# Attention by four heads and a block of keys: values and denominators on 32 columns per head, denominators in a bank of the scores

## Chip, cores, metric

One core of one Trainium2 chip. The metric is device microseconds (us) of one execution.

## The reference, cut to what matters

A graph layer and an attention layer, each with a residual and a layer norm, on a batch of 32 graphs of 512 nodes with 512 features, all in float32:

```python
def reference(x, adj, ...):                      # x (32, 512, 512), adj (512, 512)
    x = layernorm(x + gnn(x, adj))               # layer 0: deg * (x Wi + b) + adj (x Wj)
    q, k, v = heads(x @ Wq.T + bq), heads(x @ Wk.T + bk), heads(x @ Wv.T + bv)   # 8 heads of 64
    scores = einsum('bhqd,bhkd->bhqk', q, k) / 8
    scores = where(adj == 0, -inf, scores)
    attn = softmax(scores, axis=-1)
    out = einsum('bhqk,bhkd->bhqd', attn, v)
    return layernorm(x + out @ Wo.T + bo)
```

The kernel uses no maximum in the softmax. It takes exp(score), multiplies by a mask of 0 and 1, and divides the sum over keys of e·v by the sum of e (the *denominators*). A flag sum over denominators and reciprocals (`told`) decides at the end whether a safe version must run; with these inputs it does not.

## The kernel before: the parts that matter

One batch is eight *steps*. A step makes the scores of two blocks of 128 keys for one pair of heads, then the values of the step before, then some pieces of the projections of this and of neighbouring batches. The order on each engine is the order of the program. It allocates eight banks of PSUM, all in use: two for projections, two `ov` tiles of one bank, two `sc` tiles of two banks.

```python
def ov_tile():  return psum.tile([P, 512], FT, name="ov", bufs=2)
def sc_tile():  return psum.tile([P, 2, N], FT, name="sc", bufs=2)

def scores(b, hp, kc):                      # hp: pair of heads, kc: block of 128 keys
    ps = sc_tile()
    for s in range(2):
        nc.tensor.matmul(ps[:, s, :], KT[...], QT[...], start=True, stop=True)
    e = E[kc] = work([P, 2, N], "e", 4)
    nc.scalar.activation(ps, ps, AF.Exp, scale=QSCALE)
    nc.vector.tensor_tensor(e, ps, edge[...], op=OP.mult)          # the masking
...
def values(b, hp, half, kcs=None):          # two heads of 64 columns side by side
    if half == 0:
        PV[hp] = ov_tile()
    for kc in kcs or range(2 * half, 2 * half + 2):
        for s in range(2):
            c0 = hp * P + s * HD
            nc.tensor.matmul(PV[hp][s * HD:(s + 1) * HD, :], V[b][:, kc, c0:c0 + HD], E[kc][:, s, :], ...)

def sums(b, hp):                            # denominators of two heads, in an ov bank
    pl = ov_tile()
    for s in range(2):
        nc.tensor.matmul(pl[s * HD:(s + 1) * HD, :], ones[:, :HD], ES[hp][:, s, :], start=True, stop=True)
    RL[hp] = (pl, work([P, N], "rl", 1))

def rest(b, hp):                            # 4 reciprocals, scaling of the values, flag sum (tell)
    return [(invert, b, hp, c) for c in range(4)] + [(scale, b, hp), (tell, b, hp)]
...
for step in range(STEPS):
    hp, half = divmod(step, 2)
    scores(b, hp, 2 * half)
    scores(b, hp, 2 * half + 1)
    if step > 0:
        values(b, *divmod(step - 1, 2)) ; after a second half: sums(...), extra = rest(...)
    elif b > 0:
        values(b - 1, HP - 1, 1); sums(b - 1, HP - 1); extra = rest(b - 1, HP - 1)
    for f in PERIODS[n][step]:              # pieces of projections and their side work
        run(f)
        some = 0 if f[0] == 0.0 else len(extra) if step == 0 else max(1, round(f[0] / PC))
        # after a piece, `some` items of rest() are issued
```

The side work, cut from the lists of one batch: `base` is the residual base on VectorE (two inputs in SBUF), `combos`, `add_bo` and the first addition of `presum` are GpSimd's, `h_turn` is a transposition on VectorE.

```python
# phase_a(n), the end of a batch
    ... z(base, n, 0), z(combos, TX, n, xq, (3, 4)), z(combos, TA, n, aq, (3, 4)), z(base, n, 1), pc("l0", n, 1, A), k[4]]
# phase_b(n), the start of the next
    return [l0[2], *project(m, 1), l0[6], *project(m, 2), l0[7], z(add_bo, n - 1, 0), *project(m, 6), l0[4], z(stats, n, 0), ...
            l0[3], z(stats, n, 1), z(h_turn, n, 0), *project(m, 5)]
# phase_c(n), the middle
    ... q[1], k[1], z(apply, m, 0), q[2], z(apply, m, 1), z(store, m), z(h_turn, n, 1), z(combos, TH, n, h, (1, 2)), ...
```

Of the kernel before, what the change touches and what calls it, by code (L numbers as in the profile page):

```python
# [25 lines left out]
def gnn_attention_kernel(  # L26
# [16 lines left out]
):  # L43

# [114 lines left out]
    wo = load_w(work([P, NC, D], "xh", 3), woT, nc.sync)  # L159
# [17 lines left out]
    told = const.tile([P, B * HP + 1], FT, name="told")  # L177
# [31 lines left out]
    nc.gpsimd.dma_start(bv_c, bv.rearrange("(c p) -> p c", p=P))  # L209
# [4 lines left out]
    def graph_forms(part):  # L214
        if part == 3:
            nc.vector.reduce_sum(deg_c, adj_f, axis=AX.X)
        elif part == 0:
            nc.vector.tensor_tensor(adj_f, adjT, adjR.bitcast(FT), op=OP.not_equal)
        elif part == 1:
            nc.vector.reduce_sum(told[:, B * HP:], adj_f.rearrange("p c i -> p (c i)"), axis=AX.X)  # L220
            nc.vector.tensor_scalar(told[:, B * HP:], told[:, B * HP:], 2.0 * SAFE, None, op0=OP.mult)
        else:
            nc.vector.tensor_scalar(edge, adjT, 0.0, None, op0=OP.not_equal)


    RING = 8
# [5 lines left out]
    def combine(name, eng, part):  # L232
# [5 lines left out]
        if part == 0:  # L238
# [4 lines left out]
            made = ((6, s2), (5, s1), (3, s4))  # L243
        else:
# [8 lines left out]
    for name, src in (("wi", wiT), ("wj", wjT), ("wv", wvT), ("wq", wqT), ("wk", wkT), ("wo", woT)):  # L253
        WS[name, 1] = rows(src)[:, 0:2, 0:Q]
        WS[name, 2] = rows(src)[:, 2:4, 0:Q]
# [207 lines left out]
    def scores(b, hp, kc):  # L463
# [5 lines left out]
        e = E[kc] = work([P, 2, N], "e", 4)  # L469
# [4 lines left out]
    def presum(hp, half):  # L474

        if half == 0:
            ES[hp] = work([P, 2, N], "es", 1)
            nc.gpsimd.tensor_add(ES[hp], E[0], E[1])  # L478
        else:
            nc.vector.tensor_add(ES[hp], ES[hp], E[half])  # L480

    def values(b, hp, half, kcs=None):
        if half == 0:
            PV[hp] = ov_tile()
        for kc in kcs or range(2 * half, 2 * half + 2):
            for s in range(2):
                c0 = hp * P + s * HD
                nc.tensor.matmul(PV[hp][s * HD:(s + 1) * HD, :], V[b][:, kc, c0:c0 + HD], E[kc][:, s, :],  # L488
                                 start=(kc == 0), stop=(kc == NC - 1))

    def sums(b, hp):

        pl = ov_tile()
        for s in range(2):
            nc.tensor.matmul(pl[s * HD:(s + 1) * HD, :], ones[:, :HD], ES[hp][:, s, :], start=True, stop=True)  # L495
        RL[hp] = (pl, work([P, N], "rl", 1))

    def last_sums(hp, parts=(0, 2, 3)):

        if 0 in parts:  # L500
            RL[hp] = (ov_tile(), work([P, N], "rl", 1))
        for kc in parts:
            src = ES[hp] if kc == 0 else E[kc]
            for s in range(2):
                nc.tensor.matmul(RL[hp][0][s * HD:(s + 1) * HD, :], ones[:, :HD], src[:, s, :], start=(kc == 0), stop=(kc == 3))  # L505

    def invert(b, hp, part):
        pl, rl = RL[hp]
# [3 lines left out]
    def tell(b, hp):  # L512
        pl, rl = RL[hp]
        j = b * HP + hp
        nc.vector.tensor_tensor_reduce(pl, pl, rl, 1.0, 0.0, OP.add, OP.add, told[:, j:j + 1])

    def scale(b, hp, c=slice(0, N)):
        if hp % 2 == 0:
            OT[b, hp // 2] = work([P, 2, N], "oT", 3)
        nc.vector.tensor_mul(OT[b, hp // 2][:, hp % 2, c], PV[hp][:, c], RL[hp][1][:, c])  # L520

    def rest(b, hp):
        return [(invert, b, hp, c) for c in range(4)] + [(scale, b, hp), (tell, b, hp)]
# [150 lines left out]
    def last_steps():  # L674
# [4 lines left out]
        own = [(4 * GA, last_part, hp, 0) for hp in range(3)]  # L679
        return [[z(last_load), FLUSH, c[0], p[1], c[1]], [p[2], p[6]], [p[5], p[7], z(add_bo, B - 1, 0), z(add_bo, B - 1, 1)],  # L680
                [p[3], p[4], z(stats, m, 0), z(stats, m, 1)], [FLUSH, own[0], z(apply, m, 0), z(apply, m, 1), z(store, m)],
                [own[1]], [FLUSH, own[2]], []]
# [7 lines left out]
    def last_load():  # L690
        t = load_w(work([P, NC, D], "xh", 3), woT, nc.sync)
        W["wo"] = [t[:, 0:2, :], t[:, 2:4, :]]

    def last_part(hp, half=None, ic=None):
        if hp == 0:
# [5 lines left out]
        for ic in (range(2 * half, 2 * half + 2) if ic is None else (ic,)):  # L701
            nc.tensor.matmul(ACC[ic], OT[B - 1, hp // 2][:, hp % 2, ic * P:(ic + 1) * P], W["wo"][hp // 2][:, hp % 2, :],
                             start=(hp == 0), stop=(hp == HP - 1))
# [31 lines left out]
    for n in range(1, B + 1):  # L735
        b = n - 1
        extra = []
        for step in range(STEPS):
            hp, half = divmod(step, 2)
            scores(b, hp, 2 * half)  # L740
            scores(b, hp, 2 * half + 1)
            if step > 0:
                ph, phalf = divmod(step - 1, 2)
                values(b, ph, phalf)
                if phalf == 1:
                    last_sums(ph) if b == B - 1 else sums(b, ph)
                    extra = rest(b, ph)
            elif b > 0:
                values(b - 1, HP - 1, 1)
                sums(b - 1, HP - 1)  # L750
                extra = rest(b - 1, HP - 1)
            late = [(presum, hp, 0)] if half == 0 else [(presum, hp, 2), (presum, hp, 3)] if b < B - 1 else []
# [14 lines left out]
    last_sums(HP - 1, (0,))  # L767
    for kc in (2, 3):
        values(B - 1, HP - 1, 1, (kc,))
        last_sums(HP - 1, (kc,))  # L770
    for hp in range(HP - 1):
        last_part(hp, 1)
    for ic in range(NC):
        invert(B - 1, HP - 1, ic)
        scale(B - 1, HP - 1, slice(ic * P, (ic + 1) * P))
# [142 lines left out]
```

## Time and profile before

| | before |
|---|---|
| time, median of 3 | 3794.23 us (3789.84 to 3796.48) |
| TensorE busy | 99% |
| VectorE, GpSimd, ScalarE busy | 71%, 53%, 26% |
| length of one batch | 116.0 us, eight steps of 12.7 to 15.6 us |

TensorE's stream has practically no gap, so its length is the time. The prediction shows the lines. In those of a timeline the columns are the start, the length of a run of like instructions, engine, line, operation, output and inputs, shape and count; in brackets the idle time before it and what ended it. In those of groups they are busy time, the mean of one in ns, then the idle time before them and its main causes.

### The profile page before, as it was taken

The page shows a single profiled execution, that of the slowest core. Times are in us where ns is not written, and L with a number is a line of the kernel's source. Part 1 is how long each engine was busy: PE and PEld are TensorE (multiplying, and loading weights), DVE is VectorE, ACT ScalarE, POOL GpSimd, SP SyncE. Part 2 cuts the span into 40 slices and gives each one's busy share as a digit, 9 for nine tenths or more (in the row PEclk, how much of TensorE's full clock was granted, in tenths as well). Part 3 has the DMA queues.
Part 4 walks back from the last instruction along what each step waited for, and adds up shares of the span by engine and source line. Part 5 has one row for each costly group of instructions (what it writes and reads, how often), then busy time and mean ns, then how long its engine had stood idle before and what let it go on. Part 6 is the DMA issues. An engine that isn't in the chain of part 4 may idle for free.

```text
span 3793.4 us, 46029 instructions
## 1 busy us (share of the span) xinstructions
PE 3736.6 (99%) x16426; PEld 2551.5 (67%) x16426; DVE 2694.1 (71%) x3580; ACT 992.3 (26%) x1356; POOL 2027.6 (53%) x1985
## 2 busy tenths in 40 slices
PE   8999999999999999999999999999999999999997
PEld 5667666666666666666666666666666666666663
DVE  4677776777767777777777777777777777777765
ACT  2222222222222222222222222222222222222222
POOL 3556545656555565456555555654565545556533
PEclk9999999999999999999999999999999999999998
DMA  7444455445555445554445554455544555544540
GB/s 252 129 117 131 137 153 155 131 131 136 145 155 147 126 131 141 151 158 130 129 136 144 156 144 130 130 143 148 161 128 128 138 143 158 144 131 127 143 139 24
DMA packets 803720, 529.25 MB, mean 140 GB/s; under 512 B 529568, under 2 KB 626336, under 8 KB 803488
## 3 DMA queue, kind: packets, MB, share of 16 engines
q1 hardware_dynamic: 786912, 494.26, 47.7%
q10 hardware_dynamic: 16320, 31.46, 2.4%
q8 instruction: 135, 2.21, 0.2%
q14 instruction: 97, 0.79, 0.1%
q0 software_dynamic: 256, 0.53, 0.0%
HBM read 453.25 MB, written 72.88 MB: 139 GB/s over the span
## 4 chain that ended last, share of the span: by engine, by line
PE 92%; DVE 4%; POOL 1%; ACT 1%; DMA 1%; issue 1%; SPq 0%; DVEq 0%; POOLq 0%; ACTq 0%
PE mmb L413 30%; PE mma L413 30%; PE sc L467 12%; PE ov L488 11%; PE mmb L311 3%; PE mma L311 3%; PE ov L495 2%; DVE e L472 2%; POOL big L382 1%; DVE big L359 1%; ACT sc L471 1%; DVE rl L510 0%; PE ov L505 0%; DMA wq<-e 0%; DMA ring<-in_wqT_dram 0%
## 5 line engine op out<-in xcount | busy, mean ns | idle before, releaser
L471 ACT ACTIVATE sc<-sc 128x1024 f32<-128x1024 f32 x512 | 492.9, 1007 | 1617.6 <-PE sc L467 1611.7
L472 DVE TENSOR_TENSOR e<-sc,edge 128x1024 f32<-128x1024 f32 x512 | 602.5, 1218 | 262.0 <-ACT sc L471 262.0
L413 PE MATMUL mmb<-ring,big 128*128 128x256 f32 x3144 | 733.3, 382 | 3.4 <-issue 3.1
L413 PE MATMUL mma<-ring,big 128*128 128x256 f32 x3112 | 726.3, 382 | 4.2 <-ACT p L420 2.5
L413 PEld LDWEIGHTS mmb<-ring,big 128*128 128x128 f32 x3144 | 592.9, 190 | 132.9 <-issue 29.4
L413 PEld LDWEIGHTS mma<-ring,big 128*128 128x128 f32 x3112 | 586.5, 190 | 135.2 <-issue 27.0
L382 POOL TENSOR_TENSOR big<-big 128x512 f32<-128x512 f32 x376 | 507.8, 1378 | 149.2 <-DVE big L359 129.8
L194 POOL TENSOR_TENSOR xlo<-xh,xhi 128x512 fp32r<-128x512 f32 x128 | 213.9, 1680 | 605.0 <-ACT xhi L193 605.0
L467 PE MATMUL sc<-q,k 64*128 64x512 f32 x2048 | 509.9, 616 | 0.0
L488 PE MATMUL ov<-e,v 128*64 128x512 f32 x2048 | 496.0, 605 | 4.2 <-DVE oT L520 4.2
L510 DVE RECIPROCAL rl<-ov 128x128 f32<-128x128 f32 x512 | 465.4, 931 | 11.4 <-PE ov L505 5.7
L413 PE MATMUL mma<-big,ring 128*128 128x256 f32 x1808 | 431.9, 382 | 8.7 <-POOL big L382 7.7
L413 PE MATMUL mmb<-big,ring 128*128 128x256 f32 x1776 | 424.3, 382 | 8.3 <-POOL big L382 8.3
L413 PEld LDWEIGHTS mma<-big,ring 128*128 128x128 f32 x1808 | 339.1, 190 | 86.5 <-POOL big L382 14.2
L277 POOL TENSOR_SCALAR mv<-mv 128x1 f32<-128x1 f32 x256 | 49.5, 193 | 645.3 <-DVE mv L276 632.8
L413 PEld LDWEIGHTS mmb<-big,ring 128*128 128x128 f32 x1776 | 333.0, 190 | 85.1 <-POOL big L382 14.3
L478 POOL TENSOR_TENSOR es<-e 128x1024 f32<-128x1024 f32 x128 | 302.2, 2361 | 121.8 <-PE ov L495 108.7
L488 PEld LDWEIGHTS ov<-e,v 128*64 128x64 f32 x2048 | 124.5, 136 | 344.4 <-issue 271.8
L480 DVE TENSOR_TENSOR es<-es,e 128x1024 f32<-128x1024 f32 x248 | 356.0, 1436 | 0.0
L467 PEld LDWEIGHTS sc<-q,k 64*128 64x128 f32 x2048 | 176.7, 186 | 208.1 <-issue 207.8
L326 POOL TENSOR_TENSOR big<-big,deg_r 128x512 f32<-128x512 f32 x124 | 196.9, 1588 | 177.4 <-DVE big L325 177.4
L431 DVE TENSOR_TENSOR xh<-xh,mma 128x512 f32<-128x512 f32 x186 | 125.9, 677 | 195.5 <-PE mma L413 195.0
(144 smaller groups left out, 3662.9 us busy)
## 6 DMA issues: line engine op xcount, KB each, us to landing
ring<-wq SPq DMA_DIRECT2D x160, 256.0 KB, 2.9
ring<-wv SPq DMA_DIRECT2D x160, 256.0 KB, 3.1
ring<-wk SPq DMA_DIRECT2D x160, 256.0 KB, 2.8
ring<-wi SPq DMA_DIRECT2D x155, 256.0 KB, 2.8
ring<-wj SPq DMA_DIRECT2D x155, 256.0 KB, 2.6
ring<-wo SPq DMA_DIRECT2D x155, 256.0 KB, 2.7
xh<-in_x_dram SPq DMA_DIRECT2D x32, 1024.0 KB, 5.5
xa<-in_x_dram SPq DMA_DIRECT2D x124, 256.0 KB, 4.0
```

What stands on the lines that cost most here:

```text
L194: nc.gpsimd.tensor_sub(lo, xs, hi.bitcast(FT))
L311: nc.tensor.matmul(pm, parts[w][:, jc, :], adjR[:, jc, :], start=(w == 0 and jc == 0), stop=(w == 1 and jc == NC - 1))
L326: nc.gpsimd.tensor_tensor(XD[b][:, dc, :], XD[b][:, dc, :], deg_r, op=OP.mult)
L382: nc.gpsimd.tensor_tensor(dst, p, q, op=OP.subtract)
L413: nc.tensor.matmul(pm[:, c * Q:(c + 1) * Q], lhs, rhs, start=first, stop=(kc == 1 and n == len(terms) - 1), skip_group_check=True)
L467: nc.tensor.matmul(ps[:, s, :], KT[b, hp // 2][r, hp % 2, kc * P:(kc + 1) * P], QT[b, hp // 2][r, hp % 2, :], start=True, stop=True)
L471: nc.scalar.activation(ps, ps, AF.Exp, scale=QSCALE)
L472: nc.vector.tensor_tensor(e, ps, edge[:, kc:kc + 1, :].to_broadcast([P, 2, N]), op=OP.mult)
L478: nc.gpsimd.tensor_add(ES[hp], E[0], E[1])
L480: nc.vector.tensor_add(ES[hp], ES[hp], E[half])
L488: nc.tensor.matmul(PV[hp][s * HD:(s + 1) * HD, :], V[b][:, kc, c0:c0 + HD], E[kc][:, s, :], start=(kc == 0), stop=(kc == NC - 1))
L510: nc.vector.reciprocal(rl[:, c], pl[:, c])
```

## The change

The intent: handle four heads and one block of keys at a time instead of two heads and two blocks. The values of a head are made in two halves of 32 columns, so four heads sit side by side on the 128 columns, and so do their denominators. That halves the matmuls of the denominators in time, and the reciprocals and flag sums in number (a denominator now fills 32 partitions, where it filled 64). The values of four heads need both `ov` banks, so the denominators move to a bank of a score tile.

```diff
-        e = E[kc] = work([P, 2, N], "e", 4)
+        e = E[hp % 2, kc] = work([P, 2, N], "e", 4)
...
-    def values(b, hp, half, kcs=None):
-        if half == 0:
-            PV[hp] = ov_tile()
-        for kc in kcs or range(2 * half, 2 * half + 2):
-            for s in range(2):
-                c0 = hp * P + s * HD
-                nc.tensor.matmul(PV[hp][s * HD:(s + 1) * HD, :], V[b][:, kc, c0:c0 + HD], E[kc][:, s, :],
+    def values(b, g, kc):
+        if kc == 0:
+            PV[g] = [ov_tile(), ov_tile()]
+        for r in range(2):
+            for h in range(4):
+                c0 = (4 * g + h) * HD + 32 * r
+                nc.tensor.matmul(PV[g][r][32 * h:32 * h + 32, :], V[b][:, kc, c0:c0 + 32], E[h // 2, kc][:, h % 2, :],
                                  start=(kc == 0), stop=(kc == NC - 1))
-    def sums(b, hp):
-        pl = ov_tile()
-        for s in range(2):
-            nc.tensor.matmul(pl[s * HD:(s + 1) * HD, :], ones[:, :HD], ES[hp][:, s, :], start=True, stop=True)
+    def sums(g, kcs=(1,), last=1):
+        if g not in RL:
+            RL[g] = (sc_tile()[:, 0, :], work([P, N], "rl", 1))
+        for kc in kcs:
+            for h in range(4):
+                src = ES[h // 2] if kc == 1 else E[h // 2, kc]
+                nc.tensor.matmul(RL[g][0][32 * h:32 * h + 32, :], ones[:, :32], src[:, h % 2, :], ...)
...
-        return [(invert, b, hp, c) for c in range(4)] + [(scale, b, hp), (tell, b, hp)]
+        return [(invert, g, c) for c in range(4)] + [(scale, b, g, 0), (scale, b, g, 1), (tell, b, g)]
...
-            hp, half = divmod(step, 2)
-            scores(b, hp, 2 * half)
-            scores(b, hp, 2 * half + 1)
+            g, kc = divmod(step, NC)
+            scores(b, 2 * g, kc)
+            scores(b, 2 * g + 1, kc)
+            ...
+                values(pb, pg, pk)
+                if pk == NC - 1:
+                    sums(pg)
+                    extra = rest(pb, pg)
```

Cut from it: the rows of `wo` and `bv` are loaded permuted, in eight small transfers each, and all quarters of `wo` are stored in that order for the ring; a ring of weight tiles has 7 places for 8; the first addition for the denominators comes a step later, with two buffers; the last batch adds up its denominators in parts only for its last four heads.

More of the change, by code (lines that the diff above doesn't have):

```diff
@@ L158, in gnn_attention_kernel, with load_wo @@
         load_xa(1, q)
-    wo = load_w(work([P, NC, D], "xh", 3), woT, nc.sync)
+    def load_wo():
+        t = work([P, NC, D], "xh", 3)
+        for h in range(4):
+            for g in range(2):
+                nc.sync.dma_start(t[32 * h:32 * h + 32, 2 * g:2 * g + 2], woT.rearrange("(g h r d) o -> g h d r o", g=2, h=4, r=2)[g, h])
+        return t
+    wo = load_wo()
     W["wo"] = [wo[:, 0:2, :], wo[:, 2:4, :]]
@@ L174, in turned @@
         return t
-    told = const.tile([P, B * HP + 1], FT, name="told")
+    told = const.tile([P, B * 2 + 1], FT, name="told")
     adjR = const.tile([P, NC, N], FR, name="adjR")
@@ L208, in gnn_attention_kernel @@
     bv_c = const.tile([P, DC], FT, name="bv_c")
-    nc.gpsimd.dma_start(bv_c, bv.rearrange("(c p) -> p c", p=P))
+    for h in range(4):
+        for g in range(2):
+            nc.sync.dma_start(bv_c[32 * h:32 * h + 32, 2 * g:2 * g + 2], bv.rearrange("(g h r d) -> g h d r", g=2, h=4, r=2)[g, h])
     edge = const.tile([P, NC, N], BF, name="edge")
@@ L219, in graph_forms @@
         elif part == 1:
-            nc.vector.reduce_sum(told[:, B * HP:], adj_f.rearrange("p c i -> p (c i)"), axis=AX.X)
-            nc.vector.tensor_scalar(told[:, B * HP:], told[:, B * HP:], 2.0 * SAFE, None, op0=OP.mult)
+            nc.vector.reduce_sum(told[:, B * 2:], adj_f.rearrange("p c i -> p (c i)"), axis=AX.X)
+            nc.vector.tensor_scalar(told[:, B * 2:], told[:, B * 2:], 2.0 * SAFE, None, op0=OP.mult)
         else:
             nc.vector.tensor_scalar(edge, adjT, 0.0, None, op0=OP.not_equal)
-    RING = 8
+    RING = 7
     WS = {}
@@ L243, in combine @@
             made = ((6, s2), (5, s1), (3, s4))
+            if name == "wo":
+                made += ((1, a11), (2, a12))
         else:
@@ L251, in combine @@
             nc.sync.dma_start(WS[name, i], u)
-    for name, src in (("wi", wiT), ("wj", wjT), ("wv", wvT), ("wq", wqT), ("wk", wkT), ("wo", woT)):
+    for name, src in (("wi", wiT), ("wj", wjT), ("wv", wvT), ("wq", wqT), ("wk", wkT)):
         WS[name, 1] = rows(src)[:, 0:2, 0:Q]
@@ L468, in scores @@
                              QT[b, hp // 2][r, hp % 2, :], start=True, stop=True)
-        e = E[kc] = work([P, 2, N], "e", 4)
+        e = E[hp % 2, kc] = work([P, 2, N], "e", 4)
         nc.scalar.activation(ps, ps, AF.Exp, scale=QSCALE)
         nc.vector.tensor_tensor(e, ps, edge[:, kc:kc + 1, :].to_broadcast([P, 2, N]), op=OP.mult)
-    def presum(hp, half):
-        if half == 0:
-            ES[hp] = work([P, 2, N], "es", 1)
-            nc.gpsimd.tensor_add(ES[hp], E[0], E[1])
-        else:
-            nc.vector.tensor_add(ES[hp], ES[hp], E[half])
@@ L482, in values @@
-    def values(b, hp, half, kcs=None):
-        if half == 0:
-            PV[hp] = ov_tile()
-        for kc in kcs or range(2 * half, 2 * half + 2):
-            for s in range(2):
-                c0 = hp * P + s * HD
-                nc.tensor.matmul(PV[hp][s * HD:(s + 1) * HD, :], V[b][:, kc, c0:c0 + HD], E[kc][:, s, :],
-                                 start=(kc == 0), stop=(kc == NC - 1))
-    def sums(b, hp):
-        pl = ov_tile()
-        for s in range(2):
-            nc.tensor.matmul(pl[s * HD:(s + 1) * HD, :], ones[:, :HD], ES[hp][:, s, :], start=True, stop=True)
-        RL[hp] = (pl, work([P, N], "rl", 1))
@@ L498, in last_sums, with presum @@
-    def last_sums(hp, parts=(0, 2, 3)):
-        if 0 in parts:
-            RL[hp] = (ov_tile(), work([P, N], "rl", 1))
-        for kc in parts:
-            src = ES[hp] if kc == 0 else E[kc]
-            for s in range(2):
-                nc.tensor.matmul(RL[hp][0][s * HD:(s + 1) * HD, :], ones[:, :HD], src[:, s, :], start=(kc == 0), stop=(kc == 3))
-    def invert(b, hp, part):
-        pl, rl = RL[hp]
+    def presum(i, kc, eng=None):
+        if kc == 1:
+            ES[i] = work([P, 2, N], "es", 2)
+            nc.gpsimd.tensor_add(ES[i], E[i, 0], E[i, 1])
+        else:
+            (eng or nc.vector).tensor_add(ES[i], ES[i], E[i, kc])
@@ new lines, in values @@
+    def values(b, g, kc):
+        if kc == 0:
+            PV[g] = [ov_tile(), ov_tile()]
+        for r in range(2):
+            for h in range(4):
+                c0 = (4 * g + h) * HD + 32 * r
+                nc.tensor.matmul(PV[g][r][32 * h:32 * h + 32, :], V[b][:, kc, c0:c0 + 32], E[h // 2, kc][:, h % 2, :],
+                                 start=(kc == 0), stop=(kc == NC - 1))
+    def sums(g, kcs=(1,), last=1):
+        if g not in RL:
+            RL[g] = (sc_tile()[:, 0, :], work([P, N], "rl", 1))
+        for kc in kcs:
+            for h in range(4):
+                src = ES[h // 2] if kc == 1 else E[h // 2, kc]
+                nc.tensor.matmul(RL[g][0][32 * h:32 * h + 32, :], ones[:, :32], src[:, h % 2, :], start=(kc == 1), stop=(kc == last))
@@ L509, in invert, with tell @@
+    def invert(g, part):
+        pl, rl = RL[g]
         c = slice(part * P, (part + 1) * P)
         nc.vector.reciprocal(rl[:, c], pl[:, c])
-    def tell(b, hp):
-        pl, rl = RL[hp]
-        j = b * HP + hp
+    def tell(b, g):
+        pl, rl = RL.pop(g)
+        j = b * 2 + g
         nc.vector.tensor_tensor_reduce(pl, pl, rl, 1.0, 0.0, OP.add, OP.add, told[:, j:j + 1])
-    def scale(b, hp, c=slice(0, N)):
-        if hp % 2 == 0:
-            OT[b, hp // 2] = work([P, 2, N], "oT", 3)
-        nc.vector.tensor_mul(OT[b, hp // 2][:, hp % 2, c], PV[hp][:, c], RL[hp][1][:, c])
@@ L522, in rest, with scale @@
-    def rest(b, hp):
-        return [(invert, b, hp, c) for c in range(4)] + [(scale, b, hp), (tell, b, hp)]
+    def scale(b, g, r, c=slice(0, N)):
+        if (b, g) not in OT:
+            OT[b, g] = work([P, 2, N], "oT", 3)
+        nc.vector.tensor_mul(OT[b, g][:, r, c], PV[g][r][:, c], RL[g][1][:, c])
+    def rest(b, g):
+        return [(invert, g, c) for c in range(4)] + [(scale, b, g, 0), (scale, b, g, 1), (tell, b, g)]
     def store(b):
@@ L678, in last_steps @@
         c = [z(combos, TO, m, ot_quarter(m), (1, 2)), z(combos, TO, m, ot_quarter(m), (3, 4))]
-        own = [(4 * GA, last_part, hp, 0) for hp in range(3)]
+        own = [(4 * GA, last_part, c, 0) for c in range(2)]
         return [[z(last_load), FLUSH, c[0], p[1], c[1]], [p[2], p[6]], [p[5], p[7], z(add_bo, B - 1, 0), z(add_bo, B - 1, 1)],
-                [p[3], p[4], z(stats, m, 0), z(stats, m, 1)], [FLUSH, own[0], z(apply, m, 0), z(apply, m, 1), z(store, m)],
-                [own[1]], [FLUSH, own[2]], []]
+                [p[3], p[4], z(stats, m, 0), z(stats, m, 1)], [z(apply, m, 0), z(apply, m, 1), z(store, m)], [own[0]], [own[1]], []]
     def run(f):
@@ L690, in last_load, with last_part @@
     def last_load():
-        t = load_w(work([P, NC, D], "xh", 3), woT, nc.sync)
+        t = load_wo()
         W["wo"] = [t[:, 0:2, :], t[:, 2:4, :]]
-    def last_part(hp, half=None, ic=None):
-        if hp == 0:
+    def last_part(c, half=None, ic=None):
+        if c == 0:
             if half == 0:
@@ L701, in last_part @@
         for ic in (range(2 * half, 2 * half + 2) if ic is None else (ic,)):
-            nc.tensor.matmul(ACC[ic], OT[B - 1, hp // 2][:, hp % 2, ic * P:(ic + 1) * P], W["wo"][hp // 2][:, hp % 2, :],
-                             start=(hp == 0), stop=(hp == HP - 1))
+            nc.tensor.matmul(ACC[ic], OT[B - 1, c // 2][:, c % 2, ic * P:(ic + 1) * P], W["wo"][c // 2][:, c % 2, :],
+                             start=(c == 0), stop=(c == 3))
     def last_rows(ic):
@@ L738, in gnn_attention_kernel @@
         for step in range(STEPS):
-            hp, half = divmod(step, 2)
-            scores(b, hp, 2 * half)
-            scores(b, hp, 2 * half + 1)
-            if step > 0:
-                ph, phalf = divmod(step - 1, 2)
-                values(b, ph, phalf)
-                if phalf == 1:
-                    last_sums(ph) if b == B - 1 else sums(b, ph)
-                    extra = rest(b, ph)
-            elif b > 0:
-                values(b - 1, HP - 1, 1)
-                sums(b - 1, HP - 1)
-                extra = rest(b - 1, HP - 1)
-            late = [(presum, hp, 0)] if half == 0 else [(presum, hp, 2), (presum, hp, 3)] if b < B - 1 else []
+            g, kc = divmod(step, NC)
+            scores(b, 2 * g, kc)
+            scores(b, 2 * g + 1, kc)
+            pb, pg, pk = (b, *divmod(step - 1, NC)) if step > 0 else (b - 1, 1, NC - 1)
+            if pb >= 0:
+                values(pb, pg, pk)
+                if pk == NC - 1:
+                    sums(pg)
+                    extra = rest(pb, pg)
+            late = [(presum, i, kc) for i in range(2) if kc > 0]
+            if b == B - 1 and kc == 3:
+                late = [late[0], late[1] + (nc.gpsimd,)]
+            if b == B - 1 and g == 1 and kc > 1:
+                late = []
             for f in PERIODS[n][step]:
@@ L766, in gnn_attention_kernel @@
             extra = []
-    last_sums(HP - 1, (0,))
-    for kc in (2, 3):
-        values(B - 1, HP - 1, 1, (kc,))
-        last_sums(HP - 1, (kc,))
-    for hp in range(HP - 1):
-        last_part(hp, 1)
-    for ic in range(NC):
-        invert(B - 1, HP - 1, ic)
-        scale(B - 1, HP - 1, slice(ic * P, (ic + 1) * P))
-        last_part(HP - 1, ic=ic)
+    sums(1, (1, 2), 3)
+    values(B - 1, 1, 3)
+    sums(1, (3,), 3)
+    for c in range(2):
+        last_part(c, 1)
+    for ic in range(NC):
+        c = slice(ic * P, (ic + 1) * P)
+        invert(1, ic)
+        scale(B - 1, 1, 0, c)
+        scale(B - 1, 1, 1, c)
+        last_part(2, ic=ic)
+        last_part(3, ic=ic)
         if ic > 0:
             last_rows(ic - 1)
-    tell(B - 1, HP - 1)
+    tell(B - 1, 1)
     last_rows(NC - 1)
```

## The prediction

> **What bounds the kernel now.** I read, in this order, the busy shares, the chain that ended last, the groups by line, the waits, and the timelines of TensorE and VectorE over one batch. The first two:
>
> ```profile
> PE 3736.6 (99%) x16426; PEld 2551.5 (67%) x16426; DVE 2694.1 (71%) x3580; ACT 992.3 (26%) x1356; POOL 2027.6 (53%) x1985
> ...
> PE 92%; DVE 4%; POOL 1%; ACT 1%; DMA 1%; issue 1%; SPq 0%; DVEq 0%; POOLq 0%; ACTq 0%
> ```
>
> TensorE is the bound: 99% busy, 92% of the chain; VectorE has 29% to spare. Its waits hardly matter: in the waits view the largest one that returns in every batch is 8.3 us in total. So a microsecond taken from the TensorE stream is won, and a microsecond of new waiting in it is lost, whatever the other engines do. The groups that the change touches:
>
> ```profile
> L467 PE MATMUL sc<-q,k 64*128 64x512 f32 x2048 | 509.9, 616 | 0.0
> L488 PE MATMUL ov<-e,v 128*64 128x512 f32 x2048 | 496.0, 605 | 4.2 <-DVE oT L520 4.2
> L510 DVE RECIPROCAL rl<-ov 128x128 f32<-128x128 f32 x512 | 465.4, 931 | 11.4 <-PE ov L505 5.7
> ...
> L495 PE MATMUL ov<-es,ones 128*64 128x512 f32 x496 | 127.5, 592 | 1.4 <-DVE es L480 1.4
> ```
>
> The code issues 1024 score and 1024 value matmuls; each has 2048 records, so a float32 matmul is two records. A batch takes 116.0 us (from 1264.26 to the same place at 1380.28) in 8 steps; each step does two score tiles, the values of the step before, then pieces of projection. Two places in the batch that begins at 1380.28 decide my number. The step in which a batch's last denominators are made:
>
> ```profile
> 1380.28 1.99 PE L467 MATMUL sc<-q,k 64*128 64x512 f32 x8
> 1382.19 1.94 PE L488 MATMUL ov<-e,v 128*64 128x512 f32 x8
> 1383.96 1.03 PE L495 MATMUL ov<-es,ones 128*64 128x512 f32 x4
> 1384.92 3.72 PE L413 MATMUL mma<-ring,big 128*128 128x256 f32 x16
> ```
>
> Eight value records take 1.77 us start to start, 0.44 per pair: the two column halves run side by side. Four denominator records take 0.86 and about 0.1 to change to the next shape. VectorE at that moment:
>
> ```profile
> 1377.57 5.75 DVE L331 SCALAR_TENSOR_TENSOR xh<-b_r,deg_c,xh 128x512 f32<-128x512 f32 x4
> 1383.24 0.86 DVE L458 SCALAR_TENSOR_TENSOR k<-mmb,bk_c,p 128x256 f32<-128x256 f32 x2
> 1384.03 2.34 DVE L472 TENSOR_TENSOR e<-sc,edge 128x1024 f32<-128x1024 f32 x2
> ```
>
> It is behind: the masking of the first score tile ends only at about 1385.24 (1384.03 and some 1.21). Nobody waits for it now. The other place is the middle of a batch:
>
> ```profile
> 1453.66 1.99 PE L467 MATMUL sc<-q,k 64*128 64x512 f32 x8
> 1455.57 1.94 PE L488 MATMUL ov<-e,v 128*64 128x512 f32 x8
> ```
>
> ```profile
> 1453.76 0.69 DVE L442 TENSOR_TENSOR v<-mma,p 128x512 f32<-128x512 f32 x1
> 1454.37 0.68 DVE L520 TENSOR_TENSOR oT<-ov,rl 128x512 f32<-128x512 f32 x1
> 1454.97 0.69 DVE L515 CUSTOM_DVE_ANT_0 ov<-ov,rl 128x512 f32<-128x512 f32 x1
> 1455.58 0.14 DVE L515 DVE_READ_ACCUMULATOR2_ANT told<- 128x1 f32 x1
> ```
>
> The scaling and the flag sum (told) of the old heads end at 1455.72, after the new scores have begun; again nobody waits, as both sit in the ov banks, needed only by the values at 1455.57.
>
> [...] Here the starts follow each other without gaps, so I count starts, not busy time.
>
> **Part by part, per batch.** *Values*: 32 matmuls become 64, each with half the columns, four abreast instead of two: 64 records in 32 pairs become 128 in 32 fours. Change 0, if a four takes as long as a pair. *Denominators*: 8 matmuls before in pairs, 4 x 0.86 = 3.44 us; 8 after in fours, 2 x 0.86 = 1.72. **Gain 1.72 us**, all on the bound. *VectorE*: reciprocals 16 to 8 of about 0.85 start to start (-6.8 us), flag sums 4 to 2 (-1.5): 8.3 us less, on an engine with slack. Worth nothing directly. *GpSimd*: the same number of first additions, moved a step later; they finish before the e buffers are rewritten, by my reading of its queue. *Ring* of 7 for 8: its loads land in about 3 us, and 7 pieces last over 12. Nothing.
>
> *Denominators in a bank of the scores.* There are two score tiles, in rotation. The built program confirms two new waits of TensorE on VectorE. First, the denominators take the tile of the step's first scores, so they wait until its masking is done. At the batch's turn the masking ends at 1385.24, and in the last batch a matmul starts 0.12 us after the VectorE end that releases it; it could have started at 1383.96. **Loss 1.4 us.** In mid-batch the masking is done in time: 0. Second, the next step's second score tile takes the denominators' tile, so it waits for the flag sum, which the program leaves last. In mid-batch the order stays (last v, scaling, flag sum), with one more scaling of 0.61 start to start: 1455.72 + 0.61 + 0.12 = 1456.45. The second scores would start 0.96 after the first, at 1454.62. **Loss 1.8 us.** At the batch's turn the reciprocals come early, and the flag sum ends about a microsecond before it is needed: 0.
>
> Sum: -1.72 + 1.4 + 1.8 = +1.5 us in a batch. The losses occur in some 30 batches, the gain in 31: 30 x 3.2 - 31 x 1.72 = +43. The last batch adds its denominators in three parts for every head pair, now only for the last group: about 7 us of matmuls fewer, of which I keep 3, since VectorE paces those steps. The eight small loads each of wo and bv at the start lie beside the first hundred microseconds: 0. 3794 + 43 - 3 = **3834 us**.
>
> **Rivals.** (a) *The intent holds*: no new wait bites, the gain is 31 x 1.72 + 7 = 60 us, 3734. For it: VectorE loses 8 us a batch and may run ahead. Against: its backlog at 1377 to 1385 (the four residual bases) and the order in mid-batch are not touched by the change. If only one of the two waits appears, 3780 to 3792. (b) *Four column tiles do not run side by side*: with two at a time the values double, 8 x 1.77 = 14 us a batch, some 4270; with a tenth lost, 44 us, 3878. For it: nothing in this trace has four tiles or so many weight loads. Against: pairs show no cost[...]. (c) *A new wait of VectorE on GpSimd* for the e buffers, since the first addition now spans two steps; GpSimd is 53% busy and has idle stretches there. I expect none; a microsecond a batch would be 3865.
>
> **Range and chances.** If four tiles work (I say 85%), the sum of two read-off waits decides, and each may be off by half a microsecond a batch, 15 us in the total: 3790 to 3865, with (a) at the low end. If they do not, it is slower by over 2% (above 3870). So 3780 to 3880 for 8 in 10; faster 0.03, same 0.81, slower 0.16.
>
> **What would show it.** Right: value records in fours, 16 of them in about 1.77 us; denominators 0.86 for a group; in the waits view TensorE's denominators waiting for the masking, about 1.4 us some 30 times, and its scores for the flag sum, about 1.8 us some 30 times; reciprocals 256; VectorE near 64%; a batch of 117.5 us. Wrong: no such waits (then 3734), values slower than 1.77 us a step, or masking waiting for GpSimd.

## The result

| | before | after |
|---|---|---|
| median | 3792.62 us (4 runs) | 3840.47 us (3835.37 to 3842.38, 4 runs) |
| ratio | | 1.0123, 95% from 1.0106 to 1.0141 |
| batch | 116.0 us | 117.6 us |
| VectorE busy | 71% | 62% |

The change costs 1.2%, within 2%. All outputs are right. A ratio here is the mean time of one kernel's runs over the mean of the other's of the same rounds, so not quite the ratio of the medians that are quoted.

The profile of the changed kernel, first the busy shares and the shares of the chain that ended last:

```profile
PE 3695.2 (96%) x18458; PEld 2505.9 (65%) x18458; DVE 2395.5 (62%) x3202; ACT 992.5 (26%) x1356; POOL 1986.7 (52%) x1985
...
PE 81%; DVE 15%; POOL 1%; SPq 1%; issue 1%; ACT 1%; DMA 0%; DVEq 0%; POOLq 0%; ACTq 0%
```

TensorE has fewer busy microseconds (3695 for 3737) and yet the span is longer: it now waits, and VectorE has 15% of the chain where it had 4%. The groups by shape of the changed kernel (busy us, mean ns of one, idle before and its cause):

```profile
L503 PE MATMUL ov<-e,v 128*32 128x512 f32 x4096 | 498.5, 605 | 0.0
...
L513 PE MATMUL sc<-es,ones 128*32 128x512 f32 x512 | 67.4, 598 | 39.6 <-DVE e L486 39.6
...
L518 DVE RECIPROCAL rl<-sc 128x128 f32<-128x128 f32 x256 | 228.4, 924 | 3.9 <-PE sc L513 3.8
```

The values have twice the records (4096 for 2048) and the same busy time, 498.5 for 496.0 us. Busy time counts overlapping records once (4096 times 605 ns would be 2478 us), so fours of 32 columns cost what pairs of 64 cost. The denominators take 67.4 us for 127.5, and the reciprocals are half as many. So the gain is there. In the waits of TensorE (total us, times, longest) stands what eats it:

```profile
PE sc L481 <- DVE told L523: 57.1, 32, 4.4
PE sc L513 <- DVE e L486: 39.6, 31, 3.4
```

Nearly 97 us of waiting that were not there. The turn of a batch (step 0), TensorE and then VectorE:

```profile
1399.80 1.99 PE L481 MATMUL sc<-q,k 64*128 64x512 f32 x8
1401.71 1.92 PE L503 MATMUL ov<-e,v 128*32 128x512 f32 x16
1404.81 1.06 PE L513 MATMUL sc<-es,ones 128*32 128x512 f32 x8 [1.17 <-DVE e L486]
```

```profile
1397.09 5.75 DVE L345 SCALAR_TENSOR_TENSOR xh<-b_r,deg_c,xh 128x512 f32<-128x512 f32 x4
1402.76 0.86 DVE L472 SCALAR_TENSOR_TENSOR k<-mmb,bk_c,p 128x256 f32<-128x256 f32 x2
1403.55 2.34 DVE L486 TENSOR_TENSOR e<-sc,edge 128x1024 f32<-128x1024 f32 x2
```

Sixteen value records take 1.77 us from start to start, as eight did. The denominators could have begun 3.68 us into the step, as before; they begin at 5.01, after the masking of the step's first score tile, which VectorE reaches only when the four bases are through. That VectorE is late goes with what GpSimd does at the same time:

```profile
1399.02 8.65 POOL L396 TENSOR_TENSOR big<-big 128x512 f32<-128x512 f32 x6
```

The first of the four bases takes 0.71 us, the other three, beside GpSimd's work, 1.75 to 1.77 us each (the median base of e5, below, which moves two of the four to where GpSimd is idle, takes 0.74). At 0.71 each the four would be through some 3 us sooner (an estimate from these durations), which is more than the wait of 1.33 us. The kernel before has the same 5.75 us for its four bases; there nobody waited for them. The middle of the batch (step 5), TensorE and VectorE:

```profile
1473.70 1.13 PE L481 MATMUL sc<-q,k 64*128 64x512 f32 x4
1476.50 1.13 PE L481 MATMUL sc<-q,k 64*128 64x512 f32 x4 [1.67 <-DVE told L523]
1477.56 1.92 PE L503 MATMUL ov<-e,v 128*32 128x512 f32 x16
```

```profile
1474.42 1.28 DVE L528 TENSOR_TENSOR oT<-ov,rl 128x512 f32<-128x512 f32 x2
1475.61 0.69 DVE L523 CUSTOM_DVE_ANT_0 sc<-sc,rl 128x512 f32<-128x512 f32 x1
1476.22 0.14 DVE L523 DVE_READ_ACCUMULATOR2_ANT told<- 128x1 f32 x1
```

VectorE scales the values twice and comes to the flag sum last, as the list of the rest has it. The second score tile of the step is the one that held the denominators. Its scores wait until the flag sum of the old heads ends at 1476.36, and start 2.80 us into the step instead of 0.96. One batch, step by step, from the start of a step's scores to the start of the next (us):

| step | 0 | 1 | 2 | 3 | 4 | 5 | 6 | 7 |
|---|---|---|---|---|---|---|---|---|
| before | 15.20 | 14.34 | 15.20 | 14.34 | 14.29 | 14.34 | 15.56 | 12.74 |
| after | 16.62 | 14.33 | 14.33 | 14.33 | 14.30 | 16.27 | 14.69 | 12.73 |

Steps 2 and 6 lose a set of denominators each (0.87 us, twice 0.87 is 1.74). Step 0 gains the wait for the masking (+1.42), step 5 the wait for the flag sum (+1.93).

### The profile page after: what moved, and what is told of

Same layout as the page of the kernel before. It is cut to its first block, busy times and chain, and to the rows that moved or that the text cites. A ratio compares the mean times of both kernels' runs of the same rounds, so it can differ in the third digit from the quotient of the medians.

```text
span 3839.1 us, 49650 instructions
## 1 busy us (share of the span) xinstructions
PE 3695.2 (96%) x18458; PEld 2505.9 (65%) x18458; DVE 2395.5 (62%) x3202; ACT 992.5 (26%) x1356; POOL 1986.7 (52%) x1985
## 4 chain that ended last, share of the span: by engine, by line
PE 81%; DVE 15%; POOL 1%; SPq 1%; issue 1%; ACT 1%; DMA 0%; DVEq 0%; POOLq 0%; ACTq 0%
PE mma L427 27%; PE mmb L427 27%; PE sc L481 10%; PE ov L503 10%; DVE xh L345 4%; PE mmb L325 3%; PE mma L325 3%; DVE e L486 3%; DVE oT L528 1%; PE sc L513 1%; POOL big L396 1%; DVE es L494 1%; DVE big L373 1%; DVE rl L518 1%; ACT sc L485 1%
## 5 line engine op out<-in xcount | busy, mean ns | idle before, releaser
L481 PE MATMUL sc<-q,k 64*128 64x512 f32 x2048 | 521.0, 621 | 57.2 <-DVE told L523 57.1
L503 PE MATMUL ov<-e,v 128*32 128x512 f32 x4096 | 498.5, 605 | 0.0
L204 POOL TENSOR_TENSOR xlo<-xh,xhi 128x512 fp32r<-128x512 f32 x128 | 163.8, 1291 | 392.8 <-ACT xhi L203 392.8
L503 PEld LDWEIGHTS ov<-e,v 128*32 128x32 f32 x4096 | 107.8, 110 | 354.0 <-issue 354.0
L494 DVE TENSOR_TENSOR es<-es,e 128x1024 f32<-128x1024 f32 x251 | 306.8, 1223 | 0.0
L445 DVE TENSOR_TENSOR xh<-xh,mmb 128x512 f32<-128x512 f32 x186 | 126.8, 682 | 257.9 <-PE mmb L427 257.7
```

The lines of the kernel that those rows point to most:

```text
L204: nc.gpsimd.tensor_sub(lo, xs, hi.bitcast(FT))
L445: nc.vector.tensor_tensor(d, d, pm, op=OP.add)
L481: nc.tensor.matmul(ps[:, s, :], KT[b, hp // 2][r, hp % 2, kc * P:(kc + 1) * P], QT[b, hp // 2][r, hp % 2, :], start=True, stop=True)
L494: (eng or nc.vector).tensor_add(ES[i], ES[i], E[i, kc])
L503: nc.tensor.matmul(PV[g][r][32 * h:32 * h + 32, :], V[b][:, kc, c0:c0 + 32], E[h // 2, kc][:, h % 2, :], start=(kc == 0), stop=(kc == NC - 1))
```

## The experiments

Theory: the packing is worth its 1.7 us a batch, and two waits, both owed to the denominators' place in a score tile, cost 3.3. Rivals: the packing itself is worth less than counted; one of the waits is only another form of the other or of VectorE's load; something else (the ring, GpSimd) takes a part.

| run | median us | before of the same rounds | ratio (95%) |
|---|---|---|---|
| e1_flag_early | 3776.80 | 3795.03 | 0.9952 (0.9935–0.9969) |
| e2_bases_later | 3962.38 | 3795.03 | 1.0452 (1.0422–1.0483) |
| e3_both | 3896.55 | 3795.03 | 1.0279 (1.0257–1.0300) |
| e4_pairs_in_scores | 4103.51 | 3795.03 | 1.0812 (1.0794–1.0830) |
| e5_bases_step3 | 3730.95 | 3796.38 | 0.9831 (0.9818–0.9844) |
| e6_sums_later | 3740.70 | 3796.38 | 0.9853 (0.9837–0.9868) |
| e7_fours_twice | 3763.58 | 3796.38 | 0.9915 (0.9900–0.9930) |
| e8_pairs_twice | 3882.11 | 3796.38 | 1.0225 (1.0209–1.0241) |
| e9_gap_for_bases | 3910.56 | 3796.89 | 1.0288 (1.0271–1.0305) |
| e10_turn_early | 3706.83 | 3796.89 | 0.9760 (0.9744–0.9776) |
| e11_ring7 | 3797.39 | 3796.89 | 0.9999 (0.9983–1.0016) |
| e12_gap_again | 3783.63 | 3793.49 | 0.9969 (0.9952–0.9986) |

### e1_flag_early: the changed kernel, with the rest of the old heads issued faster in mid-batch

```diff
-   some = 0 if f[0] == 0.0 else len(extra) if step == 0 else max(1, round(f[0] / PC))
+   some = 0 if f[0] == 0.0 else len(extra) if step == 0 else 2 if step == NC else max(1, round(f[0] / PC))
```

> The changed kernel, with two leftover VectorE items in place of one after each piece of the middle step of a batch, so that the flag sum comes before the last projection result and not after it. Theory (two waits through the scores' bank): TensorE's wait of its scores for the flag sum, 1.84 us a batch, goes, the batch falls from 117.6 to 115.8 us and the time to about 3785 us; the wait of the denominators for the masking stays at about 40 us. Rival (the loss lies in the 32-column matmuls, their weight loads or their shape changes, and the waits only take up time that is lost anyway): TensorE's time moves elsewhere and the kernel stays near 3840 us.

The waits of TensorE in this run:

```profile
PE sc L513 <- DVE e L486: 39.6, 31, 3.4
PE sc L481 <- DVE told L523: 7.0, 2, 4.4
```

The wait for the flag sum is gone except in the last batch, the wait for the masking stands untouched, step 5 fell from 16.27 to 14.33 us, and the time went from 1.0123 to 0.9952 of before. So the two waits are independent of each other, and the second cost about 1.7% of the time, some 64 us: more than the 50.1 us that left the waits view. The timelines of step 5 show why a wait costs more than its idle time: the idle time is counted from the end of the last record (1.67), but without the wait the next record would have begun 0.17 before that end (start shifted by 2.80 − 0.96 = 1.84), and the first four score records after the wait take 1.06 to the next where they took 0.96. Together 1.93, as the step lengthened. 30 times these 0.27 are 8 us, and the rest of the 64 is near what the mean clock says (0.995 to 0.997; one thousandth is 3.8 us): in four of the changed kernel's batches the clock was at half for 3.41 us after this wait, and these batches are 1.65 us longer than the others; in e1 none is. No matmul, reciprocal or flag sum was removed here; only an order on VectorE.

### e2_bases_later and e3_both: the bases out of the way of the masking, into step 1

```diff
-     z(combos, TX, n, xq, (3, 4)), z(combos, TA, n, aq, (3, 4)), z(base, n, 1),
+     z(combos, TX, n, xq, (3, 4)), z(combos, TA, n, aq, (3, 4))] + ([z(base, n, 1)] if n == 1 else []) + [
...
-   return [l0[2], *project(m, 1), l0[6], *project(m, 2), l0[7], z(add_bo, n - 1, 0), *project(m, 6), ...
+   return [l0[2], *project(m, 1), l0[6], *project(m, 2), z(base, n, 1), l0[7], z(add_bo, n - 1, 0), *project(m, 6), ...
```

> The changed kernel, with the second pair of residual bases (two of the four VectorE operations that end just before the batch's turn) moved one step later; nothing else. Theory: VectorE's lag at the turn shrinks by about 3.4 us, the masking of the first score tile ends some 3.45 us into the step and not 4.95, the denominators' wait of 1.35 us a batch goes, and the time falls by about 40 us to about 3800 us; the wait for the flag sum stays at about 57 us. Rival (32-column matmuls are the loss): no change, 3840 us.

e3 is the same with the line of e1.

> Both edits. Theory: the two waits add, so both go: a batch of 114.3 us (116.0 of the kernel before less 1.72 us of denominators), some 3745 us, 1.2 to 1.4% faster than the kernel before. Rival (32-column matmuls, the ring of 7, or the later first additions cost the difference): not below 3790 us.

Both missed by far: 3962 and 3897 us, slower than the change itself. The wait for the masking is indeed gone (the denominators start 3.66 us into step 0), but VectorE, GpSimd and TensorE of e2 show something new in step 1:

```profile
1341.77 7.79 DVE L345 SCALAR_TENSOR_TENSOR xh<-b_r,deg_c,xh 128x512 f32<-128x512 f32 x2
1349.67 0.69 DVE L445 TENSOR_TENSOR xh<-xh,mmb 128x512 f32<-128x512 f32 x1
```

```profile
1341.22 2.38 POOL L492 TENSOR_TENSOR es<-e 128x1024 f32<-128x1024 f32 x1
1343.53 2.52 POOL L378 TENSOR_TENSOR xh<-xh,bo_r 128x512 f32<-128x512 f32 x2
1345.98 2.37 POOL L492 TENSOR_TENSOR es<-e 128x1024 f32<-128x1024 f32 x1
```

```profile
1350.41 2.07 PE L427 MATMUL mmb<-ring,big 128*128 128x256 f32 x4 [3.91 <-DVE xh L445]
```

Two bases, 0.74 us each by the median of e5, take 7.79 us together, the first of them 7.13. It ends at 1348.90, half a microsecond after GpSimd's unbroken run (1345.98 and 2.37, so 1348.35). So the base lasted not for one GpSimd instruction but for the rest of a queue of four, from 1341.77 to half a microsecond past its end. Not every run of GpSimd does so: in four batches of e2 the base was through after the first of these instructions (2.35 us), and at the turn of the changed kernel the bases beside an unbroken run take 1.75 us. What decides it is not shown. TensorE then waits 3.9 us for the additions behind the bases (27 times, 99 us in all), and its clock falls:

```profile
core 0: 3952.1 us, clock 0.978
```

The clock withheld is (1 − 0.978) × 3952 = 87 us, where the changed kernel had (1 − 0.995) × 3839 = 19. Added up against the changed kernel: waits 99 − 40, clock 87 − 19, together +127 us; measured is +122 (3962.38 − 3840.47). The two overlap, though: of the 177 us at half clock TensorE was idle for 42 (8 of 39 in the changed kernel), so some 17 us are counted twice, and about 110 of the 122 are accounted for. The clock fell at 1348.65, when TensorE had been idle for 2.15 us. In the changed kernel it fell at 1004.97, and likewise in three more batches, after the one wait of 1.67 us; in the other batches the same wait left it at full speed. What decides it is not shown. In e3, which lacks the wait for the flag sum, the time is 66 us lower than in e2: the effect of e1 (64) once more, on another base line.

### e5_bases_step3: e1, and the bases where GpSimd is idle

```diff
     (as in e2: base(n, 1) taken out of phase_a for n > 1)
-                l0[3], z(stats, n, 1), z(h_turn, n, 0), *project(m, 5)]
+                z(base, n, 1), l0[3], z(stats, n, 1), z(h_turn, n, 0), *project(m, 5)]
```

> The flag sum early, and the second pair of residual bases moved to a place where GpSimd is idle (just before the third-to-last addition of layer 0), two steps later than in the failed try where they stood behind 11 us of unbroken GpSimd work. Theory: the denominators' wait for the masking (39.6 us) goes and nothing takes its place; 3777 - 41 = about 3736 us, a batch of 114.3 us, 1.4 to 1.7% faster than the kernel before. Rival (any move of the bases costs VectorE and TensorE as much as it gives): 3770 us or more.

3730.95 us, 1.7% below before. Steps 0 and 5 are at 15.25 and 14.33 us, as before the change, and steps 2 and 6 keep their gain: the batch is 114.26 us. The bases' record, with the durations min/median/max in ns:

```profile
L345 DVE SCALAR_TENSOR_TENSOR xh<-b_r,deg_c,xh x128: 707/744/1767, 25.3 to 3575.7; 128x512 f32<-128x512 f32 x128
```

None is above 1.77 us, where in e2 and e3 the longest was 7.86 (median 1.75). e3 and e5 differ only in the place of two instructions. This is what the change was meant to give: my rival (a) had put it at 3734.

### e6_sums_later: e1, and the denominators at the turn after the first piece of projection

```diff
                 values(pb, pg, pk)
-                if pk == NC - 1:
+                late_sums = step == 0 and b < B - 1
+                if pk == NC - 1 and not late_sums:
                     sums(pg)
 ...
                     run(f)
+                    if step == 0 and 0 < b < B - 1 and f is PERIODS[n][0][0]:
+                        sums(1)
+                        extra = rest(b - 1, 1)
```

> The flag sum early, the bases where they were, and at a batch's turn the denominators' matmuls issued after the first projection piece and not right after the values: another way round the same wait, with two more changes of the array's shape in a batch at about 0.1 us. Theory: the wait for the masking goes, -41 + 6 = about 3742 us, within 10 us of the kernel with moved bases. Rival: as there, 3770 us or more.

3740.70 us. The bases stay where they were; TensorE does a piece of projection of 3.6 us first, and the masking is done by then. So the wait is one for the score tile and not for VectorE's amount of work: another order on TensorE removes it as well as another order on VectorE. It is 10 us behind e5, and some 8 of these stand in step 0: 15.52 us for e5's 15.25, in 30 batches. That is near the two further changes of shape at about 0.1 us that I had expected.

### e4_pairs_in_scores: the kernel before, with only the denominators' bank changed

```diff
-        pl = ov_tile()
+        pl = sc_tile()[:, 0, :]
```

> The kernel before with one part of the change alone: heads still in pairs of 64 columns, but the denominators written to a bank of the score tiles. Theory: no gain and only waits. Read off the trace of before: masking at the batch's turn 1.4 us, and the flag sum for the second scores of the steps after each of the four denominators 0, 4.0, 1.25 and 0.65 us; 7.3 us a batch, some 218 us, so about 4010 us (3960 to 4050). Rival (the bank is harmless and the 32-column form costs the 46 us): about 3794 us.

4103.51 us, 8.1% slower, 94 more than I expected. Waits of TensorE and a piece of its timeline:

```profile
PE sc L467 <- DVE told L515: 159.1, 92, 3.7
PE sc L495 <- DVE e L472: 36.8, 30, 3.4
```

```profile
1278.63 2.08 PE L467 MATMUL sc<-q,k 64*128 64x512 f32 x4 [3.68 <-DVE told L515]
1280.63 3.68 PE L488 MATMUL ov<-e,v 128*64 128x512 f32 x8
```

The waits are the same two, 196 us (I had worked out 218), without any packing by four: the place of the denominators alone makes them. The rest I had left out: after a wait of 3.68 us the values run at half speed (3.68 us for the eight records that took 1.94). The mean clock of the run is 0.973: (1 − 0.973) × 4099 = 111 us withheld, where before had (1 − 0.996) × 3793 = 15. Waits and clock give 196 + 96 = 292 us, less some 17 that are counted twice (TensorE was idle for 47 of the 221 us at half clock, before for 13 of 29): 275 of the 308 us. The 122 waits at the 0.27 us that one cost beyond its idle time in e1 would be 33 more; that is an estimate.

### e7_fours_twice and e8_pairs_twice: what a set of denominators costs

e7 is e5 with every ordinary set of denominators made twice, e8 is the kernel before with the same:

```diff
                     sums(pg)
+                    sums(pg)
```
```diff
         for s in range(2):
             nc.tensor.matmul(pl[s * HD:(s + 1) * HD, :], ones[:, :HD], ES[hp][:, s, :], start=True, stop=True)
+        for s in range(2):
+            nc.tensor.matmul(pl[s * HD:(s + 1) * HD, :], ones[:, :HD], ES[hp][:, s, :], start=True, stop=True)
```

> The kernel with both waits removed, each group's denominators computed twice (the second overwrites the first with the same values): the cost of fours by itself. Theory: 63 groups at 0.86 us, +54 us over the kernel without waits. Rival (four columns do not run abreast): +108 us if only two run at once.

> The kernel before with each pair's denominators of the first 31 batches computed twice: 124 pairs at 0.86 us, +107 us, about 3902 us. With the run of fours this measures the gain of the change's first part directly: 107 less 54, about 53 us.

Fours cost 32.6 us over e5, pairs 85.7 over before, each about 21 less than I expected. Their difference is 53 us, and 53 is what the prediction gives the packing (31 × 1.72 = 53.3). So the packing's worth in the denominators is measured by itself, apart from the two new waits. The shortfall is the same in both: in e7 step 0 grew by 0.86 us, but step 4 only by 0.03 (14.29 to 14.32). The middle of the batch already had slack that swallowed a set. In e5 and in the kernel before TensorE waits there for GpSimd (in e5 8.5 us on one bank and 7.9 on the other, 29 times in all); in e7 and e8 these waits are gone. The next experiment shows the place.

### e10_turn_early: e5, and the transposition that GpSimd waits for one piece earlier

```diff
-    q[1], k[1], z(apply, m, 0), q[2], z(apply, m, 1), z(store, m), z(h_turn, n, 1),
+    q[1], k[1], z(apply, m, 0), z(h_turn, n, 1), q[2], z(apply, m, 1), z(store, m),
```

> The kernel with both waits removed, and the second transposition of h issued on VectorE one piece earlier, so that the middle step of a batch isn't held up by it (GpSimd's combinations wait for it, and TensorE waits for those, 0.55 us as the waits view counts it). It tests why both doubled runs came 20 us under what I expected: if the middle step holds a hidden 0.8 us, it goes now, some 25 us, to about 3706 us. Otherwise 3731.

3706.83 us: 24 us better than e5, faster than both kernels, and 2.4% below before. TensorE in step 4, in e5 and in e10:

```profile
1309.28 1.99 PE L427 MATMUL mmb<-big,ring 128*128 128x256 f32 x8
1311.84 1.99 PE L427 MATMUL mma<-big,ring 128*128 128x256 f32 x8 [0.56 <-POOL big L396]
1313.66 1.89 PE L427 MATMUL mmb<-ring,big 128*128 128x256 f32 x8
```

```profile
1301.57 2.00 PE L427 MATMUL mmb<-big,ring 128*128 128x256 f32 x8
1303.40 1.89 PE L427 MATMUL mma<-big,ring 128*128 128x256 f32 x8
1305.13 1.89 PE L427 MATMUL mmb<-ring,big 128*128 128x256 f32 x8
```

The second group starts 1.83 us after the first where it started 2.56 us after it, and takes 1.73 to the third where it took 1.82. So a wait that the view gives as 0.56 cost 0.82 a batch, and 29 times 0.82 are the 24 us. It is also the slack of e7 and e8: 0.83 of the doubled set's 0.86 us disappeared in it. The kernel before had the same wait (8.3 and 7.7 us); the change did not make it.

### e11_ring7: the kernel before with a ring of 7

```diff
-    RING = 8
+    RING = 7
```

> The kernel before with the ring of weights cut from 8 buffers to 7, one part of the change alone. Theory: loads land in about 3 us and lead by over 12: within 0.2% of the kernel before. Rival: some of the loss is the shorter lead, up to 40 us slower.

Ratio 0.9999 (0.9983 to 1.0016): the ring is cleared.

### e9_gap_for_bases and e12_gap_again: does a base wait for a gap in GpSimd's work?

Both are e3 with GpSimd's bias additions (`add_bo`) moved later in the program, to open a gap where the bases run.

```diff
-   ... *project(m, 2), z(base, n, 1), l0[7], z(add_bo, n - 1, 0), *project(m, 6), l0[4], z(stats, n, 0), ...
+   ... *project(m, 2), z(base, n, 1), l0[7], *project(m, 6), l0[4], z(add_bo, n - 1, 0), z(stats, n, 0), ...   (e9)
+   ... *project(m, 2), z(base, n, 1), l0[7], *project(m, 6), l0[4], z(stats, n, 0), z(add_bo, n - 1, 0), ...   (e12)
```

> The failed kernel with the flag sum early and the bases one step later, in which one base ran 7.1 us behind GpSimd work without a gap; now two GpSimd additions of the output bias (2.5 us of that work) are moved a step later. Theory (the base waits for a gap in GpSimd's work[...]): the base ends about 2.4 us earlier, 4.7 us in place of 7.1, TensorE's wait for the layer-0 addition behind it falls from about 3.9 us to about 1.5 us in a batch, and with less throttling of its clock the time falls from 3897 to about 3790 (3770 to 3830). Rival (the base waits for its data): unchanged, 3897 us.

> The failed kernel with the bases one step later, as in the run before it but with the two GpSimd additions now placed behind work that GpSimd must wait for, so that its run of work really ends 2.4 us earlier (in the run before they still stood in that run, only in another order, and the base's end still followed the end of the run). Theory: the base lasts about 4.7 us in place of 7.1, TensorE's wait falls to about 1.5 us in a batch, and without the throttling of its clock the time is about 3780 (3760 to 3820). Rival (the base waits for something else): unchanged, about 3900 us.

e9 settled nothing: 3910.56 us, as slow as e3 (mean clock 0.980, in e3 0.983). The additions depend on nothing that comes late, so GpSimd did them in the same unbroken run, merely in another order; the base still ended half a microsecond after that run. In e12 the statistics are ahead of them in GpSimd's queue and hold them back. The bases of e12:

```profile
L345 DVE SCALAR_TENSOR_TENSOR xh<-b_r,deg_c,xh x128: 708/1445/5430, 25.1 to 3601.8; 128x512 f32<-128x512 f32 x128
```

Longest 5.43 us for e2's 7.86, TensorE's waits for the additions behind them 43.7 us, the mean clock 0.997, and 3783.63 us: against e3's ratio of 1.0279 it has 0.9969. Two GpSimd instructions moved out of the run took 3% of the time with them. So it is GpSimd's run and not VectorE's load that holds the bases here. Why this run can hold them over several instructions, and the run at the turn does not, is not shown.

## Why the prediction was right

**Fours cost what pairs cost** (85% given): right. Sixteen records in 1.77 us, 498.5 us busy for 496.0. Before the result it was my estimate from the pairs (eight records in 1.77 us); the trace of the kernel before has no 32-column matmul.

**Denominators −1.72 us a batch**: right. Steps 2 and 6 are 0.87 us shorter each, 1.74; e7 and e8 give 53 us for the whole run, as computed.

**Wait for the masking 1.4**: right. Step 0 is 1.42 us longer, and the waits view has 39.6 us in 31 times (1.28 each; 1.17 in most). e5 and e6 remove it in two ways.

**Wait for the flag sum 1.8**: right, slightly short in size. The start of the second scores moved by 1.84 us, as worked out from VectorE's order; the step lengthened by 1.93, because I had not counted the slower restart (1.06 us for four records that took 0.96), nor that waits cost clock (3.41 us at half speed in each of four batches). (The 0.12 us that I took from the last batch for the delay of a released matmul lies within the 0.05 to 0.15 that the trace has there.) The sum per batch is 1.61 us where I had 1.5, and the total +48 us (3840.47 − 3792.62) where I had +40.

**Rival (a)**: the intent, at 3734, fell for the change itself but is the time of e5 (3731), where both waits are gone. That supports the argument that the change's balance is the gain less just these two waits. The 65 us of e5 against before are 31 × 1.74 = 54 from the batches; of the other 11 I had "about 7" from the last batch, and the trace of e5 has 6.8 there (91.3 us from its first scores to the end, for 98.1 before).

**VectorE near 64%, nothing directly**: 62%. Its 299 us less work (2694.1 − 2395.5) moved nothing by itself; its order moved 109 us (3840 to e5's 3731).

**Ring and GpSimd, nothing**: the ring by e11; no masking waited for GpSimd in the changed kernel. (The waits view names GpSimd for 29 waits of 0.9 us of the masking, 25.5 us; but the exponential that the masking needs ends at the same moment, and the kernel before has an idle time of 0.8 us in the same place under ScalarE.) But I had taken from the profile only that GpSimd was 53% busy; that one of its unbroken runs would hold a base for 7.13 us I did not foresee, and it spoilt my expectations of e2 and e3. I also read TensorE's waits as hardly worth a look, at 8.3 us for the largest: the view has one wait in two lines, a bank each (8.3 and 7.7 us, 29 times in all), and e10 got 24 us from it.

**Last batch −3**: the traces have −6.9, from its first scores to the end (98.1 us before, 91.2 after), although it shows new waits (4.40 us for the flag sum before a score tile, and others of 2 to 3 us). The size is that of the 7 us that I had worked out; no run tests whether they are the cause. The four batches at half clock, 6.6 us longer together, I did not have. That the total came within 8 us of mine is in part luck: these two go opposite ways.

**Rivals (b) and (c)**: four tiles do run side by side (sixteen records of 605 ns in 1.77 us), and no wait on GpSimd for the e buffers appears.

What stays open: what in the last batch gave the 6.9 us, and why a base lasts to the end of one run of GpSimd (7.13 us in e2) and not of another (1.75 us at the turn). Denominators in a bank of their own, with the packing by four, were not tried: the eight banks that the kernel allocates are all in use.

## What to carry to other kernels

A buffer that changed its bank took over the waits of that bank's other users here (196 us of them in e4): before moving one, list who must have finished reading (here the masking of the step's first scores) and who comes next (here the next step's second scores), and read from the timeline when those ends fall. Work that was removed from an engine with slack gained nothing here, while the order of the work left on it cost more than the change saved; so look for the last item in its queue that the bound engine now needs. And where VectorE has work beside a long run of GpSimd, look at the lengths of its instructions: here the cost stood there (a base of 7.13 us in e2, for 0.74 as the median of e5), not in a wait that the views name.

## Hardware figures of this case

- A base of 0.74 us (median of e5) took 7.13 us in e2, beside four GpSimd instructions in a row; beside another unbroken run, at the turn of the changed kernel, 1.75 us.
- After a wait of 1.67 or 1.68 us TensorE's clock was at half for 3.41 us, in four batches of the changed kernel.
- Four tiles of 32 columns ran abreast in float32: sixteen records in 1.77 us, the time of eight records of 64 columns in the kernel before.
- Weight-load records took 190, 136 and 110 ns for 128, 64 and 32 columns (means of the kernel before and, for 32, of the changed one).
- From the denominators to the next shape it took about 0.1 us: four records 0.96 us to the next start, where four of the values took some 0.86.
- A short wait of TensorE cost 0.26 to 0.27 us beyond its idle time (0.56 shown, 0.82 lost in e5; 1.67 shown, 1.93 lost in step 5 of the changed kernel).
